# Small results two to a PSUM bank, and turns of rows at other places, in a fused attention and mixture-of-experts kernel

## The chip, the cores and the metric

The kernel runs on one core of a Trainium2 chip. The metric is the device time of one execution in microseconds (us); the time of a kernel is the median over its runs. In what follows PE is TensorE, DVE is VectorE, ACT is ScalarE, POOL is GpSimd and SP is SyncE; a "turn" is a transpose on PE.

## The reference

`x` is 2048 tokens (16 blocks of 128) of 256 numbers; the context has the same shape. First a gated attention with 16 heads in a sliding window, then a gated mixture of 8 experts, of which each token takes two. Cut to what matters:

```python
x = x + tanh(g_xattn) * attention(layernorm(x), ctx, ctx)
x = x + tanh(g_ffn) * moe(layernorm(x))

# attention: q = (x Wq + bq) / 4, k, v from ctx; a block of 128 queries sees
# its own block and the one before, inside a band of 129 keys
scores = where(valid, q @ k.T, -inf)
out = (softmax(scores) @ v) @ Wo + bo

# moe
xn = layernorm(x) * ln_gamma + ln_beta
probs = softmax(clip(xn @ Wr.T, -1e4, 1e4))
top_p, top_i = top_k(probs, 2)          # each token goes to two experts
# tokens in order take a slot each of their experts, at most 640 an expert
buf[e, slot] = xn[token]
g, u = split(buf[e] @ W12[e].T)         # 1024 + 1024
y = (silu(g) * u) @ W3[e].T             # back to 256
out[token] += y[slot] * weight          # for both of its experts
```

## The kernel before

All arithmetic is in float32 but for a few bfloat16 masks. The order of work on each engine is written by hand (a manual schedule): instructions stand on an engine in the order in which the Python code issues them, and the tile framework adds only the semaphores. PSUM, PE's output memory, has eight banks of 2 KB a partition. During the attention they are dealt out like this: `ps_m` has two banks that go round among nearly all small results (tag "m"), `ps_s` has two tiles of two banks for scores, `ps_t` has one tile of two banks for turned probabilities (`pp` of L524, read by ACT's `prT` copy, L526). After the attention loop another pool, `pf`, takes the place of `ps_s` and `ps_t`.

**Head.** Context, queries, keys and values of the first blocks are made. `unit_v(0, (0, 1))` makes the first values: its result `pv` (L437) is a tile of `ps_m`, and ACT's copies of the keys (`keo`, L370) free those banks.

**The attention loop** (L896 on) goes over the blocks t = 0 to 15. A round interleaves the attention of block t with later steps of earlier blocks and earlier steps of later ones. What follows is the middle of a round, with the functions that the change touches:

- DVE: `summed` (L513, the second half of the sums of exponents), `inverted` (L517, reciprocal `rd`), `divided(t-1)` (L567, `oT` from the products of the round before and `rb`), then the maxima (`largest`, L494) of block t+1.
- PE: `scores(t+1)`, `turned(t, 0)` (L524), `facing(t-2)` (L625: turns the normalised block `xn` into `pxt`; ACT copies it to `x2T`, L629), `attended(t-1)` (L575: the output projection `pp`; DVE adds it to `x_all`, L583, and takes the statistics of the second layernorm).
- `ranked` and `placed` for some rounds (L749: the slots of a group of routed blocks), then one of `units(t)`: `one()` makes keys, values, queries or turned blocks of later groups (L360, L437, L395).
- PE: `turned(t, 1)`, `routed(t-2)` (L635: router logits `pl` from `x2T`; DVE clips them into `logits`, L642), `by_head(t)` (L533: `prd`, turned reciprocals; DVE copies them to `rdT`), `weighted(t)` (L546 and L557: probabilities times values, `po`).
- `scaled(t-1)`: the second layernorm on POOL and DVE (L595, L602, L611, L612), which ends in `xn`; then POOL sends four of the waiting rows to their slots with indirect DMAs (L807).

Before the change every one of `pxt`, `pp`, a unit's result, `pl`, `prd` is a tile of its own in the two banks of `ps_m`, so each waits for the read of the result two before it.

**Head of the experts.** After the loop the last blocks are routed, while PE already makes gate and up products of the first expert (`gate_or_up`, L1009; `silu`, L1018; `hidden`, L1023) from its first three tiles of rows, which were fetched inside the loop. `ranked` (L749) follows DVE's choice of the top two (L734), and `send` issues the last indirect DMAs.

**Experts** are taken in the order 2, 0, 5, 1, 3, 4, 6, 7 (loop at L1397). An expert has up to five tiles ("slots") of 128 rows, and a switch on its count picks an arm of code with `m` slots. The first expert (`FIRST`) has m = 5 in this run: its down products (`down`, L1305 on) for slots 0 to 2 come first, then `slots_turned` (L1141) turns slots 3 and 4 (L1146, copied by ACT at L1158), then `up` (L1166) makes their gate and up products. The second and the third expert have m = 2 (`up`), the other five use `seven` (L1234, a scheme with seven products of half-matrices in place of eight), which needs sums of the turned rows (`row_sums`, L1226 on, DVE).

A down product of one slot is eight matmuls with two halves (`down_parts`, L1305): it yields after four matmuls, after eight, and then `weigh` (L1325) scales by the router's weight on DVE. At the boundary between two experts slots 0 to 3 of the next expert are turned (L1146, copied by ACT at L1151), then comes a half of a down product of the old expert, then the turn of slot 4 and `row_sums`, and then the remaining three halves:

```python
next(downs[0])
if i + 1 < E:
    slots_turned(nxt[0], bufT, 4, 5, halves=True)
    row_sums(bufT, bs)
for k, parts in enumerate(downs):
    ...
```

For the first expert `downs` has one product only. The weighted rows are added to the result in HBM by indirect DMAs of POOL (L1340), four copies move the result to the output.

Of the kernel before, what the change touches and what calls it, by code (L numbers as in the profile page):

```python
# [20 lines left out]
P = 128  # L21
D = 256
# [9 lines left out]
E = 8  # L32
# [22 lines left out]
def flamingo_block(  # L55
# [252 lines left out]
    with tc.tile_pool(name="grp", bufs=2) as grp, tc.tile_pool(  # L308
# [118 lines left out]

            return evict

        def unit_v(g, bs):  # L430
            cg, vp = ctxs[g], vps[g % 2]
            vpv = vp.rearrange("p b (k a) (h d) -> p b k a h d", a=2, h=2)
            n = len(bs)
            pv = ps_m.tile([P, n, D], F32, tag="m", name=f"pv_{g}_{bs[0]}")
            for i, b in enumerate(bs):
                for c in range(DC):
                    nc.tensor.matmul(  # L437
                        pv[:, i, :],
                        lhsT=cg[:, c, b * P : (b + 1) * P],
                        rhs=wv_sb[:, c, :],  # L440
                        start=(c == 0),
                        stop=(c == DC - 1),
                    )
# [68 lines left out]
        def summed(t, q, sc):  # L512
            nc.vector.tensor_reduce(sc[3][:, q, :, :], sc[2][q], AX.X, ALU.add)  # L513

        def inverted(t, sc):
            rd = small.tile([P, H], F32, tag="rd", name=f"rd_{t}")
            nc.vector.reciprocal(rd, sc[3].rearrange("p q i j -> p (q i j)"))  # L517
            return rd
# [8 lines left out]
            return prT  # L527


        def by_head(t, rd):  # L530

            prd = ps_m.tile([H, P], F32, tag="m", name=f"prd_{t}")
            nc.tensor.transpose(prd, rd, ident)  # L533
            rdT = wk.tile([H, P], F32, tag="rdT", name=f"rdT_{t}")
            nc.vector.tensor_copy(rdT, prd)
            return rdT
# [18 lines left out]
        def divided(t, po, rd):  # L555
            for oc in range(DC):
                nc.tensor.matmul(  # L557
                    po[:, 1, oc, :],
                    lhsT=sel[:, oc, :, :, :].rearrange("k s a d -> k (s a d)"),
                    rhs=rd,  # L560
                    start=True,
                    stop=True,
                )
            rb = wk.tile([P, DC, P], F32, tag="rb", name=f"rb_{t}")
            nc.scalar.copy(rb, po[:, 1, :, :])
            oT = wk.tile([P, DC, P], F32, tag="oT", name=f"oT_{t}")
            nc.vector.tensor_tensor(oT, po[:, 0, :, :], rb, ALU.mult)  # L567
            return oT

        def attended(t, oT):  # L570
            g, b = divmod(t, GB)
            x1 = xs[g][:, b, :]
            pp = ps_m.tile([P, D], F32, tag="m", name=f"pp_{t}")
            for c in range(DC):
                nc.tensor.matmul(  # L575
                    pp,
                    lhsT=oT[:, c, :],
                    rhs=wo_sb[:, c, :],
                    start=(c == 0),
                    stop=(c == DC - 1),  # L580
                )

            nc.vector.scalar_tensor_tensor(x1, pp, tgx[:, 0:1], x1, ALU.mult, ALU.add)  # L583
# [11 lines left out]
            nc.gpsimd.tensor_tensor(rs, ve, minus_half[:, 0:1], ALU.pow)  # L595
            return mv, rs
# [21 lines left out]
                )  # L618
            return normed

        def facing(t):
            g, b = divmod(t, GB)
            pxt = ps_m.tile([P, DC, P], F32, tag="m", name=f"pxt_{t}")
            for c in range(DC):
                nc.tensor.transpose(  # L625
                    pxt[:, c, :], xn2s[g][:, b, c * P : (c + 1) * P], ident
                )
            x2T = wk.tile([P, DC, P], F32, tag="x2T", name=f"x2T_{t}")
            nc.scalar.copy(x2T, pxt)  # L629
            return x2T  # L630

        def routed(t, x2T):
            pl = ps_m.tile([P, E], F32, tag="m", name=f"pl_{t}")
            for c in range(DC):
                nc.tensor.matmul(  # L635
                    pl,
                    lhsT=x2T[:, c, :],
                    rhs=wr_sb[:, c, :],
                    start=(c == 0),
                    stop=(c == DC - 1),  # L640
                )
            nc.vector.tensor_scalar(  # L642
                logits[:, t, :], pl, CLAMP, -CLAMP, ALU.min, ALU.max
            )
# [199 lines left out]
        with tc.manual_schedule(engines={PE, ACT, DVE}):  # L844
# [18 lines left out]
                normed_x(0, bs, *m)  # L863
            nc.vector.tensor_scalar(bqs, bq_sb, HD**-0.5, None, ALU.mult)
            nc.vector.tensor_copy(bvb, bv_sb.unsqueeze(2).to_broadcast([P, DC, P]))
            unit_v(0, (0, 1))()
            unit_k(1, 0)()
            unit_t(0)()
            normed_x(1, every, *measured(1, every))
# [26 lines left out]
            for t in range(NB):  # L896
# [4 lines left out]
                if t == 0:  # L901
                    prTs = [turned(t, 0, sc)]
                    unit_t(1)()
                    scn = scores(t + 1)
                    summed(t, 1, sc)
                    rdT = by_head(t, inverted(t, sc))
                    for q in range(2):
                        largest(t + 1, q, scn)
                else:
                    summed(t, 1, sc)  # L910
                    rd = inverted(t, sc)
                    oT = divided(t - 1, *pend)
                    if nxt:
                        scn = scores(t + 1)
                        for q in range(2):
                            largest(t + 1, q, scn)
                    prTs = [turned(t, 0, sc)]
                if t >= 2:
                    x2T = facing(t - 2)
                if t >= 1:  # L920
                    norm = attended(t - 1, oT)
                if routing is not None:
                    place = placed(*ranked(*routing))
                    next(place)
# [6 lines left out]
                    g, b = divmod(t - 1, GB)  # L931
                    mv_rs = measured(g + 2, [b])
                prTs.append(turned(t, 1, sc))
                if t >= 2:
                    routed(t - 2, x2T)
                if t >= 1:
                    rdT = by_head(t, rd)
                po = weighted(t, prTs, rdT)
                pend = po, rdT
                if t == 13:  # L940
# [98 lines left out]

            t = NB - 1  # L1040
            oT = divided(t, *pend)
            x2T = facing(t - 1)
            gate_or_up(0, 0)
            norm = attended(t, oT)
            silu(0)
            routed(t - 1, x2T)
            gate_or_up(0, 1)
            c = chosen(t - 4, 4)
            next(c)
# [7 lines left out]
            hidden(1)  # L1057
            silu(2)
            routing = next(c)
            x2T = facing(t)  # L1060
            gate_or_up(2, 1)
            routed(t, x2T)
            ranks = ranked(*routing)
            hidden(2)
            for _ in placed(*ranks):
# [14 lines left out]
            gate_or_up(5, 0)  # L1080
            routing = next(c)
            hidden(4)
            ranks = ranked(*routing)
            count = counted("count")
            for _ in placed(*ranks):
                pass
            for u in of_tiles(*routing[0:2]):
                send(*u)
            gate_or_up(5, 1)
            silu(5)  # L1090

            over = small.tile([P, E], F32, name="over", bufs=1)
# [12 lines left out]
    with tc.tile_pool(name="ffn", bufs=2, reuse_waits="tile") as ffn:  # L1105
# [271 lines left out]
        with tc.manual_schedule(engines={PE, ACT, DVE}):  # L1377
# [19 lines left out]
            for i, e in enumerate(ORDER):  # L1397
# [9 lines left out]
                for case in tc.Switch(nw, arms(e), hint=f"width_{e}"):  # L1407
# [24 lines left out]
                            slots_turned(rows, buf_a, s, min(s + 2, m, AT))  # L1432
                        up(w12, buf_a, None, 0, min(m, AT) * P)
                    for k, s in enumerate([*range(2, min(m, AT)), 0]):
                        down(e, w3, hT, rows, left, ysb, s, k)
                    if m == 2:

                        nc.tensor.matmul(
                            pys[1][:, 0:E], lhsT=ones, rhs=ones[:, 0:E], start=True, stop=True
                        )  # L1440
                    if m > AT:
                        slots_turned(rows, buf_b, AT, m, off=AT)
                        up(w12, buf_b, hT, AS, m * P, off=AS)
                    list(ahead)
                    for s in range(AT, m):
# [11 lines left out]
                downs = [down_parts(*args, 0, 1)] if e != FIRST else []  # L1457
                downs.append(down_parts(*args, 1, 0))
                next(downs[0])
                if i + 1 < E:  # L1460
                    slots_turned(nxt[0], bufT, 4, 5, halves=True)
                    row_sums(bufT, bs)
                for k, parts in enumerate(downs):
                    if k > 0:
                        next(parts)
                    next(parts)
                    if k + 1 < len(downs):
                        next(parts, None)
# [99 lines left out]
```

## Time and profile before

| | us |
|---|---|
| median of 3 runs (lowest to highest) | 528.17 (528.05 to 528.65) |
| profiled execution | 526.98 |
| its span, first to last instruction | 525.3 |
| PE busy in the span | 493.4 (94%) |
| DVE busy | 301.9 (57%) |
| ACT busy | 227.5 (43%) |
| POOL busy | 156.1 (30%) |
| granted TensorE clock, mean | 0.996 of full speed |

The profile is of one execution, 1.19 us below the median. Times in it are counted from the span's start. In lines of the timeline the first two numbers are start and duration in us, the name before the arrow is the tile written and those behind it are read; x8 joins eight instructions in a row; brackets at the end give the idle time of that engine just before, and what ended it. A name such as `ctx` or `x_all` can stand for a later tile that took over its memory. The attention loop lies at about 21 to 198, the head of the experts at 198 to 232, the experts at 232 to 516.

### The profile page before, as it was taken

How to read it: one execution, taken by the hardware profiler on the slowest of the kernel's cores; microseconds unless marked ns; L12 is line 12 of the kernel's file. 1: busy time of each engine (PE TensorE's matmuls, PEld its weight loads, DVE VectorE, ACT ScalarE, POOL GpSimd, SP SyncE). 2: the span in 40 equal slices, each digit the busy share in tenths (PEclk: the TensorE clock that was granted, in tenths of full speed). 3: DMA queues.
4: the chain of work that ended last, by engine and by line, in shares of the span. 5: the costliest groups of instructions: out<-in, count | busy, mean ns of one | idle time of the engine just before them, and what ended most of it. 6: DMA issues, size and time to landing. Idle time of an engine off the chain costs nothing.

```text
span 525.3 us, 8420 instructions
## 1 busy us (share of the span) xinstructions
PE 493.4 (94%) x2935; PEld 371.1 (71%) x2935; DVE 301.9 (57%) x748; ACT 227.5 (43%) x620; POOL 156.1 (30%) x187
## 2 busy tenths in 40 slices
PE   8998999999998889999999999999999999999993
PEld 4655666666666666578878888898677867877682
DVE  6578788877687966624453656373464256334510
ACT  3677777668665664311221242351441144024400
POOL 5133422254216255600222223323110211034212
PEclk9999999999999999999999999999999999999998
DMA  8999610011002116230477583572910250023301
GB/s 253 317 273 386 208 41 1 2 41 62 2 1 104 53 42 241 87 125 2 111 231 204 147 279 69 130 218 29 304 18 12 35 143 10 3 36 82 149 12 40
DMA packets 38410, 59.17 MB, mean 113 GB/s; under 512 B 3617, under 2 KB 33825, under 8 KB 36193
## 3 DMA queue, kind: packets, MB, share of 16 engines
q1 hardware_dynamic: 30704, 47.71, 27.3%
q0 software_dynamic: 7056, 10.24, 10.3%
q8 instruction: 42, 0.69, 0.5%
q14 instruction: 64, 0.52, 0.3%
q10 hardware_dynamic: 544, 0.00, 0.1%
HBM read 39.40 MB, written 19.34 MB: 112 GB/s over the span
## 4 chain that ended last, share of the span: by engine, by line
PE 70%; issue 8%; DVE 7%; ACT 6%; DMA 5%; POOL 1%; SPq 0%; ACTq 0%; POOLq 0%; DVEq 0%
PE py L1314 14%; PE pg L1258 9%; PE pu L1258 7%; PE pg L1172 4%; DMA acc_d<-ysb,tok 4%; PE pp L524 4%; PE pu L1172 4%; PE ps L482 3%; PE pq L411 3%; ACT prT L526 3%; PE po L546 3%; PE bank L1258 3%; PE ps L474 3%; PE pk L360 3%; DVE mx L494 2%
## 5 line engine op out<-in xcount | busy, mean ns | idle before, releaser
L1340 POOL DMA_INDIRECT acc_d<-ysb,tok x35 | 56.1, 1602 | 190.7 <-DMA acc_d<-ysb,tok 73.0
L1314 PE MATMUL py<-w,hT 128*128 128x256 f32 x432 | 97.1, 379 | 0.0
L1314 PEld LDWEIGHTS py<-w,hT 128*128 128x128 f32 x432 | 80.9, 190 | 11.2 <-DVE hT L1269 0.5
L505 ACT ACTIVATE pr<-ps,mx 128x128 f32<-128x128 f32 x256 | 69.5, 405 | 2.6 <-DVE mx L494 2.5
L1258 PE MATMUL pg<-bufT,w 128*128 128x320 f32 (+1 forms) x160 | 50.6, 398 | 0.2
L526 ACT COPY prT<-pp 128x1024 f32<-128x1024 f32 x32 | 32.6, 1019 | 40.0 <-PE pp L524 30.5
L513 DVE TENSOR_REDUCE sm<-pr 128x8 f32<-128x1024 f32 x32 | 38.9, 1217 | 14.1 <-ACT pr L505 14.1
L494 DVE TENSOR_REDUCE mx<-ps 128x8 f32<-128x1024 f32 x32 | 37.6, 1216 | 7.9 <-PE ps L482 7.7
L524 PE MATMUL pp<-ident,pr 128*128 128x128 f32 x256 | 34.6, 278 | 2.2 <-ACT prT L526 1.7
L807 POOL DMA_INDIRECT slot_d<-xn,slot x32 | 31.6, 988 | 14.5 <-issue 7.7
L524 PEld LDWEIGHTS pp<-ident,pr 128*128 128x128 f32 x256 | 28.2, 141 | 10.6 <-issue 6.0
L1258 PEld LDWEIGHTS pg<-bufT,w 128*128 128x128 f32 x160 | 28.0, 189 | 10.6 <-ACT vp L1292 2.3
L1151 ACT COPY bufT<-bank 128x256 f32<-128x256 f32 (+1 forms) x42 | 11.4, 347 | 51.8 <-PE bank L1146 45.1
L595 POOL TENSOR_TENSOR rs<-ve,minus_half 128x1 f32<-128x1 f32 x16 | 8.9, 556 | 78.7 <-DVE ve L591 78.6
L546 PE MATMUL po<-prT,vp 128*32 128x128 f32 x512 | 22.3, 277 | 7.1 <-DVE logits L642 2.9
L1289 ACT ACTIVATE vp<-pu 128x320 f32<-128x320 f32 (+1 forms) x40 | 15.8, 396 | 29.1 <-PE pu L1258 14.5
L1328 DVE TENSOR_SCALAR ysb<-py,rows 128x256 f32<-128x256 f32 x20 | 9.6, 482 | 31.2 <-PE py L1314 28.6
L1278 ACT COPY pg<-pg 128x320 f32<-128x320 f32 (+1 forms) x20 | 7.3, 367 | 42.7 <-PE pg L1258 36.8
L1184 ACT ACTIVATE vp<-pg 128x256 f32<-128x256 f32 x24 | 9.2, 383 | 37.2 <-PE pg L1172 34.9
L546 PEld LDWEIGHTS po<-prT,vp 128*32 128x32 f32 x512 | 14.7, 109 | 13.6 <-DVE logits L642 6.4
L1294 DVE TENSOR_TENSOR pu<-pg,vp 128x320 f32<-128x320 f32 (+1 forms) x20 | 8.9, 446 | 17.5 <-PE pg L1258 14.0
L482 PE MATMUL ps<-keo,qT 32*128 32x256 f32 x256 | 18.3, 400 | 0.0
(217 smaller groups left out, 967.2 us busy)
## 6 DMA issues: line engine op xcount, KB each, us to landing
w<-in_w12T_dram SPq DMA_DIRECT2D x16, 1024.0 KB, 8.3
w<-in_w3T_dram SPq DMA_DIRECT2D x8, 1024.0 KB, 12.3
slot_d<-zrow SPq DMA_DIRECT2D x1, 5300.0 KB, 26.6
rows<-slot_d SPq DMA_DIRECT2D x7, 662.5 KB, 4.2
x_all<-in_x_dram SPq DMA_DIRECT2D x4, 512.0 KB, 6.3
acc_d<-x_all SPq DMA_DIRECT2D x4, 512.0 KB, 4.6
out_dram<-acc_d SPq DMA_DIRECT2D x4, 512.0 KB, 8.1
ctx<-in_ctxT_dram SPq DMA_DIRECT2D x3, 512.0 KB, 6.1
```

The lines of the kernel that those rows point to most:

```text
L482: nc.tensor.matmul(pss[s // 2][:, s % 2, 2 * oc : 2 * oc + 2, :], lhsT=qT[rows, oc, b * P : (b + 1) * P], rhs=keo[rows, oc, b, :, :], star ...
L494: nc.vector.tensor_reduce(mx, sc[0][q], AX.X, ALU.max, negate=True)
L505: nc.scalar.activation(prs[q][:, i, j, :], pss[q][:, i, j, :], AF.Exp, bias=mxs[q][:, i, j : j + 1],)
L513: nc.vector.tensor_reduce(sc[3][:, q, :, :], sc[2][q], AX.X, ALU.add)
L524: nc.tensor.transpose(ppt[:, i, j, :], sc[2][q][:, i, j, :], ident)
L526: nc.scalar.copy(prT, ppt)
L546: nc.tensor.matmul(po[32 * s : 32 * s + 32, 0, oc, :], lhsT=vp[:, b, h, :], rhs=prTs[s // 2][:, s % 2, 2 * oc + a, :], start=(a == 0), sto ...
L807: d = nc.gpsimd.indirect_dma_start(out=slot_d, out_offset=bass.IndirectOffsetOnAxis(ap=slot[:, k, t : t + 1], axis=0), in_=xn2s[g][:, b, : ...
L1172: nc.tensor.matmul(ps, lhsT=w12[:, c, f0 : f0 + P], rhs=(buf[:, c, :, 0 : n // 2] if len(buf.shape) == 4 else buf[:, c, lo - off : hi - off]),
L1258: nc.tensor.matmul(to, lhsT=lhs[:, i * P : (i + 1) * P], rhs=rhs[:, 0:n], start=start, stop=True, skip_group_check=not start,)
L1314: mm = nc.tensor.matmul(py, lhsT=h, rhs=w3[:, f, :], start=(f == 0), stop=(f == FC - 1),)
L1340: nc.gpsimd.indirect_dma_start(out=acc_d, out_offset=bass.IndirectOffsetOnAxis(ap=tok[:, s : s + 1], axis=0), in_=ysb[:, s, :], in_offset= ...
```

## The change

1. `unit_v(0, (0, 1))` takes its PSUM tile from `ps_t` (tile `pv_0`).
2. In the loop, `facing` and `attended` write into two halves of one bank (`large_bank`), `routed` and `by_head` into two parts of another (`small_bank`). Matmuls and reads are separate functions now: first both groups of matmuls, then both reads.
3. At t = 15 `divided(14)` stands ahead of the last `summed` on DVE.
4. `gate_or_up(5, 1)` stands ahead of the last `ranked` and `counted`.
5. For the first expert with m > 3, the turn of slots 3 and 4 stands between the two halves of the down product of slot 0.
6. Between experts, where there are two down products, all of the first (with its `weigh`) stands ahead of the turn of slot 4 and `row_sums`; the second follows.

```diff
-        def unit_v(g, bs):
+        def unit_v(g, bs, pv=None):
...
-            pv = ps_m.tile([P, n, D], F32, tag="m", name=f"pv_{g}_{bs[0]}")
+            if pv is None:
+                pv = ps_m.tile([P, n, D], F32, tag="m", name=f"pv_{g}_{bs[0]}")
...
-            unit_v(0, (0, 1))()
+
+            pv = ps_t.tile([P, DC, GT], F32, tag="t", name="pv_0")
+            unit_v(0, (0, 1), pv[:, 0, :].rearrange("p (b d) -> p b d", d=D))()
...
+        def small_bank(t):
+            both = ps_m.tile([P, BANK], F32, tag="m", name=f"small_{t}")
+            return both[:, 0:E], both[0:H, P : 2 * P]
...
+        def large_bank(t):
+            both = ps_m.tile([P, 2, D], F32, tag="m", name=f"large_{t}")
+            return both[:, 0, :].rearrange("p (c t) -> p c t", c=DC), both[:, 1, :]
...
-            pp = ps_m.tile([P, D], F32, tag="m", name=f"pp_{t}")
...
-            pxt = ps_m.tile([P, DC, P], F32, tag="m", name=f"pxt_{t}")
...
-            pl = ps_m.tile([P, E], F32, tag="m", name=f"pl_{t}")
...
                 else:
+                    if not nxt:
+                        oT = divided(t - 1, *pend)
                     summed(t, 1, sc)
                     rd = inverted(t, sc)
-                    oT = divided(t - 1, *pend)
                     if nxt:
+                        oT = divided(t - 1, *pend)
                         scn = scores(t + 1)
...
-                if t >= 2:
-                    x2T = facing(t - 2)
                 if t >= 1:
-                    norm = attended(t - 1, oT)
+                    pxt, pp = large_bank(t)
+                    if t >= 2:
+                        facing(t - 2, pxt)
+                    attended(t - 1, oT, pp)
+                    if t >= 2:
+                        x2T = facing_read(t - 2, pxt)
+                    norm = attended_read(t - 1, pp)
...
-                if t >= 2:
-                    routed(t - 2, x2T)
                 if t >= 1:
-                    rdT = by_head(t, rd)
+                    pl, prd = small_bank(t)
+                    if t >= 2:
+                        routed(t - 2, x2T, pl)
+                    by_head(t, rd, prd)
+                    if t >= 2:
+                        routed_read(t - 2, pl)
+                    rdT = by_head_read(t, prd)
...
+            gate_or_up(5, 1)
             ranks = ranked(*routing)
             count = counted("count")
...
-            gate_or_up(5, 1)
             silu(5)
...
-                        down(e, w3, hT, rows, left, ysb, s, k)
+                        parts = down_parts(e, w3, hT, rows, left, ysb, s, k)
+                        next(parts)
+                        if s == 0 and m > AT:
+                            slots_turned(rows, buf_b, AT, m, off=AT)
+                        for _ in parts:
+                            pass
...
                     if m > AT:
-                        slots_turned(rows, buf_b, AT, m, off=AT)
                         up(w12, buf_b, hT, AS, m * P, off=AS)
...
                 next(downs[0])
+                if len(downs) > 1:
+                    next(downs[0])
+                    next(downs[0], None)
                 if i + 1 < E:
                     slots_turned(nxt[0], bufT, 4, 5, halves=True)
                     row_sums(bufT, bs)
-                for k, parts in enumerate(downs):
-                    if k > 0:
-                        next(parts)
-                    next(parts)
-                    if k + 1 < len(downs):
-                        next(parts, None)
+                if len(downs) > 1:
+                    next(downs[1])
+                next(downs[-1])
```

More of the change, by code (lines that the diff above doesn't have):

```diff
@@ L527, in turned, with by_head, by_head_read @@
             return prT
-        def by_head(t, rd):
-            prd = ps_m.tile([H, P], F32, tag="m", name=f"prd_{t}")
+        def small_bank(t):
+            both = ps_m.tile([P, BANK], F32, tag="m", name=f"small_{t}")
+            return both[:, 0:E], both[0:H, P : 2 * P]
+        def by_head(t, rd, prd):
             nc.tensor.transpose(prd, rd, ident)
+            return prd
+        def by_head_read(t, prd):
             rdT = wk.tile([H, P], F32, tag="rdT", name=f"rdT_{t}")
@@ L568, in divided, with attended @@
             return oT
-        def attended(t, oT):
-            g, b = divmod(t, GB)
-            x1 = xs[g][:, b, :]
-            pp = ps_m.tile([P, D], F32, tag="m", name=f"pp_{t}")
+        def large_bank(t):
+            both = ps_m.tile([P, 2, D], F32, tag="m", name=f"large_{t}")
+            return both[:, 0, :].rearrange("p (c t) -> p c t", c=DC), both[:, 1, :]
+        def attended(t, oT, pp):
             for c in range(DC):
@@ L581, in attended, with attended_read @@
                 )
+            return pp
+        def attended_read(t, pp):
+            g, b = divmod(t, GB)
+            x1 = xs[g][:, b, :]
             nc.vector.scalar_tensor_tensor(x1, pp, tgx[:, 0:1], x1, ALU.mult, ALU.add)
@@ L619, in scaled, with facing @@
             return normed
-        def facing(t):
+        def facing(t, pxt):
             g, b = divmod(t, GB)
-            pxt = ps_m.tile([P, DC, P], F32, tag="m", name=f"pxt_{t}")
             for c in range(DC):
@@ L627, in facing, with facing_read @@
                 )
+            return pxt
+        def facing_read(t, pxt):
             x2T = wk.tile([P, DC, P], F32, tag="x2T", name=f"x2T_{t}")
@@ L630, in facing, with routed @@
             return x2T
-        def routed(t, x2T):
-            pl = ps_m.tile([P, E], F32, tag="m", name=f"pl_{t}")
+        def routed(t, x2T, pl):
             for c in range(DC):
@@ L641, in routed, with routed_read @@
                 )
+            return pl
+        def routed_read(t, pl):
             nc.vector.tensor_scalar(
@@ L905, in flamingo_block @@
                     summed(t, 1, sc)
-                    rdT = by_head(t, inverted(t, sc))
+                    rdT = by_head_read(t, by_head(t, inverted(t, sc), small_bank(t)[1]))
                     for q in range(2):
@@ L1041, in flamingo_block @@
             oT = divided(t, *pend)
-            x2T = facing(t - 1)
+            x2T = facing_read(t - 1, facing(t - 1, large_bank("last")[0]))
             gate_or_up(0, 0)
-            norm = attended(t, oT)
+            norm = attended_read(t, attended(t, oT, large_bank("out")[1]))
             silu(0)
-            routed(t - 1, x2T)
+            routed_read(t - 1, routed(t - 1, x2T, small_bank("last")[0]))
             gate_or_up(0, 1)
@@ L1059, in flamingo_block @@
             routing = next(c)
-            x2T = facing(t)
+            x2T = facing_read(t, facing(t, large_bank("end")[0]))
             gate_or_up(2, 1)
-            routed(t, x2T)
+            routed_read(t, routed(t, x2T, small_bank("end")[0]))
             ranks = ranked(*routing)
```

## The prediction, made before the run

> **What bounds the kernel now.** I read the busy shares and the chain that ended last on the page, then the list of what TensorE (PE) waited for, and then the timeline around each of those waits that the diff touches.
>
> ```profile
> PE 493.4 (94%) x2935; PEld 371.1 (71%) x2935; DVE 301.9 (57%) x748; ACT 227.5 (43%) x620; POOL 156.1 (30%) x187
> ...
> PE 70%; issue 8%; DVE 7%; ACT 6%; DMA 5%; POOL 1%; SPq 0%; ACTq 0%; POOLq 0%; DVEq 0%
> ```
>
> PE is busy 94% of the 525.3 us span, and the chain lies on it for 70%. The change adds and removes no matmul, and no DMA changes its place in SP's or POOL's queue, so it can only give back PE's 32 us of idle time, or add to them. The waits of PE (total us, times, longest):
>
> ```profile
> PE po L546 <- DVE logits L642: 2.9, 4, 0.8
> PE bank L1146 <- ACT bufT L1151: 1.9, 2, 1.3
> ...
> PE pp L575 <- DVE oT L567: 1.1, 1, 1.1
> ...
> PE pv L437 <- ACT prT L526: 0.9, 1, 0.9
> PE pg L1172 <- ACT ctx L1158: 0.7, 1, 0.7
> PE rank L749 <- DVE top L734: 0.7, 1, 0.7
> PE pv L437 <- ACT keo L370: 0.7, 1, 0.7
> PE rank L749 <- ACT x2T L629: 0.6, 2, 0.3
> PE pt L395 <- ACT x2T L629: 0.6, 2, 0.3
> PE pv L437 <- ACT x2T L629: 0.6, 2, 0.3
> ```
>
> Each of these lines answers to one part of the diff; together they are 10.7 us. The question is how much comes back: a wait that goes is worth only what the next event lets through. In what follows, gains are differences of start times in the profiled execution (526.98 us, 1.68 more than its span; 1.19 below the median of 528.17).
>
> **1. First value product in a bank of its own.** `pv` starts at 10.42 after waiting for the `keo` copy (L370); PE was free at 9.59, and its weights had landed at 9.04 (DMA issue at 3.14, 5.9 to landing). So it can start 0.83 earlier. The following `pk` at 12.26 reuses a bank already copied out, and ACT, which must copy `vp`, is busy with `keo` to 11.71 (8.93 + 2.78), the earliest end of the new `pv` being 11.6. I take 0.85 (the extra 0.02 is a launch gap), bounds 0.6 to 0.95.
>
> **2. Two results in one bank, in the loop.** Facing (`pxt`, L625) and attended (`pp`, L575) now share a bank, both matmul groups first, then both reads; routed (`pl`) and by_head (`prd`) likewise. The small result behind them therefore finds a free bank without waiting for the x2T copy. In exchange the x2T copy on ACT waits until attended's matmuls end, and the read of `pp` on DVE (L583) waits for the x2T copy. Queued behind these are ACT's exponents (L505) and the next `prT` copy, and on DVE the statistics and logits. Round t=2:
>
> ```profile
> 48.57 1.03 PE L575 MATMUL pp<-wo_sb,oT 128*128 128x256 f32 x4
> 49.46 0.38 ACT L629 COPY x2T<-pxt 128x256 f32<-128x256 f32 x1
> ...
> 49.79 0.47 DVE L583 SCALAR_TENSOR_TENSOR x_all<-pp,tgx,x_all 128x256 f32<-128x256 f32 x1
> ...
> 50.80 1.01 ACT L526 COPY prT<-pp 128x1024 f32<-128x1024 f32 x1
> ...
> 52.00 1.08 PE L546 MATMUL po<-prT,vp 128*32 128x128 f32 x32 [0.82 <-DVE logits L642]
> ```
>
> L575 ends at 49.60, so x2T starts at about 49.64 instead of 49.46: 0.18 later. L583 then starts at about 50.07 instead of 49.79: 0.28 later. DVE has 0.43 of idle time ahead of L513 at 52.88, which hides that; without this cover it would cost 0.28 a round. What of the 0.82 that `po` waited for logits? The line says that it goes, but the `prT` copy on which `po` also depends ends only at 51.81 and will end 0.18 later. So `po` starts at about 52.04: no gain but 0.04 lost, and the same at t=3 and t=4 (62.20, 72.39): -0.1 in all, bounds -0.6 to 0.
>
> PE's waits of 0.29 for x2T occur at t=5, 6, 7, 9, 10 and 11. At t=6 and 10 (`pv`) and 11 (`rank`) nothing else is late: 3 x 0.29 = 0.87. At t=5 and 9 the second half of `pt` lies in the shared bank and waits for L583, which ends 0.4 after the wait that goes; at t=7 `pk` does so, and L583 stands behind 2.34 us of maxima (L494). There I take nothing. At t=12 `pv` waited 0.87 (start 162.13) because the `prT` copy was late at 160.79; `pv` needs it no more: 0.75, but only 0.29 if that copy comes on time in the next execution. Sum of the loop: 0.87 + 0.75 - 0.1 = 1.52, bounds 0.3 to 2.4.
>
> [...]
>
> **3. Division ahead of the last sum (t=15).**
>
> ```profile
> 192.48 1.10 PE L575 MATMUL pp<-wo_sb,oT 128*128 128x256 f32 x4 [1.15 <-DVE oT L567]
> ...
> 195.40 0.57 POOL L595 TENSOR_TENSOR rs<-ve,minus_half 128x1 f32<-128x1 f32 x1
> ...
> 198.11 0.44 PE L625 MATMUL pxt<-ident,xn 128*128 128x128 f32 x2
> ```
>
> `oT` needs `rb` (ends 191.06) and not the sum L513 (190.55 to 191.77), so L575 can start at about 191.5: 0.95 earlier. But the end of this stretch is `facing` at 198.11, which waits for `xn` from POOL, and POOL's chain (195.40, `h` 196.51, `xn` 197.31 to 198.03) stands behind four sends (190.51 to 195.37) that are anchored in POOL's earlier work and don't move. All of PE's 0.95 turns into waiting at 198.11: 0, bounds 0 to 0.95.
>
> **4. A gate product ahead of the ranks.** `rank` at 216.74 waited 0.69 for DVE's top-2; four gate matmuls fill it now. But PE then reaches the down product earlier, and there ACT and DVE resume at 225.8 (after 4.98 and 5.48 idle, with inputs ready at 221.6 and 222.9, while indirect sends are under way). PE's matmuls on the last two hidden tiles, at 226.57 and 227.0, were just met (weight load waited 0.15). If these stay where they are, about 0.6 is waited there: 0.1, bounds -0.5 to 0.7. The ranks come 1.5 later, POOL's sends for them start at 221.74, and their slots were ready at 218.47: that covers it.
>
> **5. First expert's last slot turned within the down product.** The turn at 230.91 (0.60), ACT's copy (231.59, 0.58) and then `pg` at 232.23 with 0.72 waited stood behind one another. Sixteen down matmuls fill 223.98 to 230.91, 0.433 each. Now the turn comes after half a product, 4 x 0.433 = 1.73 earlier, with the rows landing at 228.57 by the neighbouring load; the copy is done under the other half. Gain 0.72 + 0.15 of gaps = 0.87, bounds 0.4 to 0.95.
>
> **6. Turns between experts.** A down matmul is two records here (x8 is four matmuls).
>
> ```profile
> 272.29 1.89 PE L1314 MATMUL py<-w,hT 128*128 128x256 f32 x8
> ...
> 275.45 0.44 PE L1146 MATMUL bank<-ident,rows 128*128 128x128 f32 x2 [1.27 <-ACT bufT L1151]
> ```
>
> ```profile
> 330.79 0.38 PE L1146 MATMUL bank<-ident,rows 128*128 128x128 f32 x2
> ...
> 331.01 5.35 PE L1314 MATMUL py<-w,hT 128*128 128x256 f32 x24
> ...
> 332.95 0.48 DVE L1231 TENSOR_TENSOR wq_sb<-bufT,x_all 128x320 f32<-128x320 f32 x1
> ```
>
> Four matmuls after 272.29 end at 274.02; slot 4's turn came at 275.45 because ACT's copies started late (274.75, after 3.62 idle): 1.43 lost. At 298.16 it is 0.83 in the same way. Eight matmuls (3.46) last past both: 1.43 + 0.83 = 2.26. The price is the cover behind: the row sums must be ready when the next expert starts. At 330.79 they took to 333.43, 2.64 after slot 4's turn; with the weighing (L1328, 0.5) now ahead of them 3.14, against 0.22 + 3.46 = 3.68 of remaining matmuls. It fits with 0.54 to spare: no cost, bounds 0 to 1.73 a boundary if not.
>
> **Sum.** 0.85 + 1.52 + 0 + 0.10 + 0.87 + 2.26 = 5.60. From 526.98 that is 521.4, and with the 1.19 to the median **522.6 us**. The tail after the last matmul (516.3 to 525.3) is untouched.
>
> **Rivals.**
> - *Only the experts count (0.21).* The loop and the head are paced by ACT's and POOL's chains, so parts 1 to 4 come to nothing; 5 and 6 leave 3.13: 525.0. For it: the four zeros that I already found. Against: at t=6, 10 and 11 I see no later event.
> - *More comes back (0.09).* POOL's and DVE's lateness at 195.4 and 225.8 belongs to one execution, and parts 3 and 4 give 0.95 + 0.6, with 0.87 at t=5, 7 and 9: 8.0, so 520.1.
> - *Slower (0.10).* Slot 4's copies run late at the five boundaries ahead of a `seven` expert, as ACT's copies did by 2 us or more at 274.75. It decides once the sums take more than 3.68 after the turn. With 2 us of lateness the cost is 2.0 - 0.54 = 1.46, five times 7.3: 1.7 worse than before, 529.9. Against it: at 331.21 ACT copied slot 4 at once.
> - *It doesn't do what it says (0.05).* The added waits (0.18 on ACT, 0.28 on DVE, some 13 rounds, up to 3.6) and a lost 1 to 2 in part 4 eat the gain: 528.
>
> **How the numbers follow.** The forecast keeps 0.55, with its own range of 521 to 524. A range of 520.0 to 526.1 takes in the first two rivals and leaves out the last two. Measurements of this kernel can tell about 0.2% (1.06 us) from no change: faster 0.85, same 0.05, slower 0.10.
>
> **What would show it.** Right: in the waits of PE the lines of `bank` for `bufT`, `pg` for `ctx`, `pv` for `keo` and those for x2T are gone; `po` at t=2 to 4 now waits for `prT`; a new wait stands at the `facing` of 198 and at the products of 226. Wrong: a new wait of the first matmul of `seven` for DVE's sums, or ACT idle ahead of the last `bufT` copies, or a loop round longer than before at t=2 to 11.

## The result, and the profile after

The changed kernel took 521.77 us (median of 4 runs, 521.42 to 522.34), beside 528.35 for the kernel before in the same runs: ratio 0.9877, 95% interval 0.9859 to 0.9894, so 6.5 us or 1.2% faster. The forecast was 522.6 with a range of 520.0 to 526.1. The profiled execution took 522.01 (span 520.3), 4.97 less than that of before; of the two, that of before happened to lie 1.4 under its median and that of after 0.2 above it.

The page after: PE is as busy as before, in a shorter span (15 of its records are missing from this trace).

```profile
PE 491.1 (94%) x2920; PEld 372.2 (72%) x2935; DVE 303.2 (58%) x748; ACT 228.6 (44%) x620; POOL 157.1 (30%) x187
```

What PE waited for (total us, times, longest):

```profile
PE po L554 <- ACT prT L527: 6.6, 15, 0.8
...
PE pt L395 <- DVE x_all L598: 1.1, 2, 0.5
PE large_last L639 <- POOL xn L627: 0.9, 1, 0.9
PE py L1345 <- DVE x_all L1054: 0.8, 1, 0.8
PE pk L360 <- DVE x_all L598: 0.5, 1, 0.5
```

Every line that was named as going is gone: `bank` for `bufT`, `pg` for `ctx`, `pv` for `keo`, all those for x2T, `po` for logits, and `rank` for DVE. What came in their place is the point of this view. The first line (15 waits, 6.6 us) says that the copies of probabilities on ACT (`prT`) now end last in nearly every round. The second and the last are waits that the shared bank adds (in rounds 5, 9 and 7), the third and the fourth the places where the division's and the gate product's gains stop.

Because all these executions have nearly the same work, the time can be followed by the starts of the same matmuls in both traces (before minus after, cumulative):

| up to | us gained |
|---|---|
| first scores (21.04 before) | 0.30 |
| last scores of the loop (179.68) | 2.34 |
| first gate product (198.39) | 2.18 |
| first down product (223.98) | 3.11 |
| first product on rows 3 and 4 (232.23) | 2.58 |
| second expert (257.60) | 2.69 |
| third expert (280.91) | 4.18 |
| fourth expert (304.10) | 4.93 |
| end of the span | 4.97 |

The wait that the shared bank adds, in round 2 (columns: start, duration, instruction, idle before it and its cause). x2T starts just after the projection ends, and the read of the projection after x2T:

```profile
48.29 1.03 PE L585 MATMUL large<-wo_sb,oT 128*128 128x256 f32 x4
49.35 0.37 ACT L646 COPY x2T<-large 128x256 f32<-128x256 f32 x1
49.76 0.48 DVE L598 SCALAR_TENSOR_TENSOR x_all<-large,tgx,x_all 128x256 f32<-128x256 f32 x1 [0.16 <-ACT x2T L646]
```

With the 0.28 by which this trace runs ahead here, that is 49.63 and 50.04 on the clock of before; the prediction had 49.64 and 50.07. Between experts the four copies still start late, but PE has eight matmuls to do (x16, two records each) and meets the next turn without waiting:

```profile
269.60 3.62 PE L1345 MATMUL py<-w,hT 128*128 128x256 f32 x16
...
271.53 1.20 ACT L1182 COPY bufT<-bank 128x256 f32<-128x256 f32 x4 [3.08 <-issue]
...
273.06 0.38 PE L1177 MATMUL bank<-ident,rows 128*128 128x128 f32 x2
```

### The profile page after: what moved, and what is told of

Read it like the earlier page. It is cut to its first block, busy times and chain, and to the rows that moved or that the text cites. A ratio compares the mean times of both kernels' runs of the same rounds, so it can differ in the third digit from the quotient of the medians.

```text
span 520.3 us, 8402 instructions
## 1 busy us (share of the span) xinstructions
PE 491.1 (94%) x2920; PEld 372.2 (72%) x2935; DVE 303.2 (58%) x748; ACT 228.6 (44%) x620; POOL 157.1 (30%) x187
## 4 chain that ended last, share of the span: by engine, by line
PE 71%; ACT 7%; issue 7%; DVE 7%; DMA 5%; POOL 1%; SPq 0%; POOLq 0%; DVEq 0%; ACTq 0%
PE py L1345 15%; PE pg L1289 9%; PE pu L1289 7%; PE pu L1203 4%; PE pg L1203 4%; PE pp L525 4%; DMA acc_d<-ysb,tok 4%; ACT pr L506 4%; PE ps L483 3%; PE pk L360 3%; ACT prT L527 3%; PE bank L1289 3%; DVE mx L495 2%; PE pv L438 2%; PE pq L411 2%
## 5 line engine op out<-in xcount | busy, mean ns | idle before, releaser
L554 PE MATMUL po<-prT,vp 128*32 128x128 f32 x512 | 23.7, 277 | 7.3 <-ACT prT L527 6.6
L475 PE MATMUL ps<-causal,ident_b 128*128 128x512 bf16 x49 | 15.8, 382 | 2.0 <-ACT pr L506 1.4
```

The costliest lines, as they stand in the source:

```text
L554: nc.tensor.matmul(po[32 * s : 32 * s + 32, 0, oc, :], lhsT=vp[:, b, h, :], rhs=prTs[s // 2][:, s % 2, 2 * oc + a, :], start=(a == 0), sto ...
```

## The experiments

Times are medians; each ratio is to the kernel before on the same chip, with its 95% interval. Effects here are 0.1 to 1%, so I read the ratio for the sum and the trace for the place. Of each edit the main lines are shown. "The stretch" is the time from PE's first down product to its first product on rows 3 and 4 (223.98 to 232.23 before, 8.25).

**1. The turns of rows alone** (parts 5 and 6 of the change's list). The edit to the kernel before is the hunks of the change for these parts, of which the main lines are:

```diff
+                        if s == 0 and m > AT:
+                            slots_turned(rows, buf_b, AT, m, off=AT)
...
+                if len(downs) > 1:
+                    next(downs[0])
+                    next(downs[0], None)
                 if i + 1 < E:
                     slots_turned(nxt[0], bufT, 4, 5, halves=True)
```

> The kernel before with parts 5 and 6 alone (turns of rows within and between experts' products). Theory (each wait of PE that goes is worth the difference of start times): 0.87 within the first expert plus 1.43 and 0.83 between experts, 3.1 us less than before, about 525.2. Rival (the lateness at the first expert belongs to ACT's and DVE's pause near 226 and stays): the 2.26 between experts alone.

Measured: ratio 0.9936 (0.9911 to 0.9962), 3.4 us. The stretch is 7.34 beside 8.23 in *head_only*, which has the old order there: 0.89. The wait ahead of the product on rows 3 and 4, before and here (the turn, then the product):

```profile
232.23 1.13 PE L1172 MATMUL pg<-ctx,w 128*128 128x256 f32 x4 [0.72 <-ACT ctx L1158]
```

```profile
227.22 0.60 PE L1146 MATMUL bank<-ident,ctx 128*128 128x128 f32 x4
...
229.38 1.03 PE L1172 MATMUL pg<-ctx,w 128*128 128x256 f32 x4
```

From the second expert to the fourth it took 44.51 against 46.50: 1.99. How late the copies of the old order are differs from execution to execution (45.99 in *shared_only*, which has the old order too). The theory holds; the rival's 2.26 without the first expert's part does not, for that part shows its 0.89.

**2. The shared banks alone** (part 2), with all of its hunks, of which two lines are:

```diff
+                    pxt, pp = large_bank(t)
...
+                    pl, prd = small_bank(t)
```

> The kernel before with part 2 alone (two results to a bank in the loop). Theory (the gain of a round is the gap of starts, 0.46 to 0.56 in rounds 6, 10, 11, 0.74 in round 12, minus 0.25 in rounds 5 and 9): 2.0 us by the last scores of the loop, of which at most 0.3 is lost by the first expert, so 1.7 to 2.0 less than before. Rival (the loop's end is paced by POOL's sends, so the gain turns into waiting for the last normalised blocks): under 0.8 less.

Measured: ratio 0.9951 (0.9933 to 0.9970), 2.6 us. From the first to the last scores 154.76, and 156.56 to 156.57 in each of the three kernels of this set that have the old loop: 1.81 gained, 1.7 of it still there at the first gate product. The rival (under 0.8) is out.

**3. The head alone** (part 1).

```diff
-            unit_v(0, (0, 1))()
+            pv = ps_t.tile([P, DC, GT], F32, tag="t", name="pv_0")
+            unit_v(0, (0, 1), pv[:, 0, :].rearrange("p (b d) -> p b d", d=D))()
```

> The kernel before with part 1 alone (the first value product in a bank of its own). Theory (a wait of 0.83 goes, and the loads come when they come): 0.5 to 0.85 less than before; in the profile no idle time of PE ahead of the first pv, whenever the first keys begin. Rival (the 0.30 seen in the changed kernel is all that there is, since ACT's copies are next): 0.3 or less, with ACT late for the following key copies.

Measured: ratio 0.9990 (0.9971 to 1.0008), 0.5 us and not told from none. In the trace PE no longer idles ahead of `pv`, but the first keys began at 6.39, later than in the others, and `pv` came at 10.21. Over all profiles the first scores start at 20.48 on average in nine executions with part 1 (20.05 to 20.78) and at 20.88 in four without (20.68 to 21.04): 0.4, between theory and rival. But these executions differ in when the first keys are done, and the part on why the prediction was right shows that with this taken out the theory's 0.83 is there.

**4. Division and gate product alone** (parts 3 and 4).

```diff
+                    if not nxt:
+                        oT = divided(t - 1, *pend)
                     summed(t, 1, sc)
...
+            gate_or_up(5, 1)
             ranks = ranked(*routing)
```

> The kernel before with parts 3 and 4 alone (division ahead of the last sum; a gate product ahead of the ranks). Theory (0.95 of the division is given back at the facing product behind POOL's sends, 0.69 of the ranks is mostly given back at the down product, where ACT and DVE resume late): 0 to 0.4 less than before. Rival (the waits go for good): 1.0 to 1.6 less.

Measured: ratio 0.9978 (0.9962 to 0.9994), 1.2 us. Half of each, of theory and rival: from the last scores to the first gate product 19.15 against 19.19 in *head_only*, so the division gives 0.04; from there to the first down product 24.65 against 25.60, and the stretch unchanged (8.22 against 8.23), so the gate product gives 0.95 and keeps it. What the theory relied on there, that ACT and DVE resume late, didn't happen in this set of runs at all (below).

**5. The changed kernel again, as a base.**

> The changed kernel as it is, on the chip of this set of runs, as the base for the three beside it. Theory (the parts add up): 2.0 to 2.6 of the shared banks, 3.1 to 3.4 of the turns, 0.3 to 0.5 of the head and about 1.0 of the ranks make 6.4 to 7.5 us less than the kernel before, and the profile shows no pause of ACT and DVE near 222, so that the gate product's gain is kept. Rival (the division and the gate product run into POOL's sends and the down product): 5.5 or less.

Measured: 520.94, ratio 0.9890 (0.9867 to 0.9913), 5.8 us (4.6 to 7.0): between theory and rival, and the interval reaches into both. The four kernels with parts alone add up to 7.6, but on another chip and each known to about 1 us only. The wait at the facing product (0.85) and a pause of ACT and DVE near 222 are both back.

**6. One send fewer in round 14.**

```diff
-                    pace(normed, 4)
+                    pace(normed, 3 if t == 14 else 4)
```

> The changed kernel with three sends of rows in place of four in round 14, the fourth left for the end. Theory (PE's wait of 0.86 for the last but one normalised block is made by the four sends ahead of it on POOL, and it is where the division's gain went): the wait goes and the kernel is 0.7 to 0.9 us faster than the changed one. Rival (DVE's statistics or the later sends take their place, or the wait comes back at the next normalised block): the same within 0.2.

Measured: ratio 0.9866 (0.9844 to 0.9889), 0.7 us under the base of its set by the medians (1.3 by the ratios), which the intervals alone can't tell from none. The trace can:

```profile
192.19 0.57 POOL L610 TENSOR_TENSOR rs<-ve,minus_half 128x1 f32<-128x1 f32 x1 [0.40 <-issue]
...
194.89 0.44 PE L639 MATMUL large_last<-ident,xn 128*128 128x128 f32 x2
```

POOL stands idle ahead of the norm's first step (0.40) instead of sending, PE's wait is gone, and the way from the last scores to the first gate product is 17.98 instead of 18.76. So the four sends were where the division's gain went; the division and one send fewer together bring 0.8, the division alone nothing. One send fewer without the division was not run.

**7. Banks not shared in rounds 5, 7 and 9**, on top of 6.

```diff
-                    pxt, pp = large_bank(t)
+                    if t in (5, 7, 9):
+                        pxt = ps_m.tile([P, DC, P], F32, tag="m", name=f"pxt_{t}")
+                        pp = ps_m.tile([P, D], F32, tag="m", name=f"pp_{t}")
+                    else:
+                        pxt, pp = large_bank(t)
```

> The kernel pace_3 with separate banks for the two large results in rounds 5, 7 and 9, where the next product needs the second of the two banks. Theory (there sharing costs 0.25 in rounds 5 and 9 and nothing in 7, since the next product waits for the projection's read, which waits for the x2T copy): 0.5 us faster than pace_3. Rival (the probabilities' copies on ACT set the pace of these rounds anyway): the same as pace_3 within 0.2.

Measured: ratio 0.9870 (0.9847 to 0.9892), no difference to *pace_3* by time. In the trace rounds 5 and 9 take 11.19 each, as before the change, and 11.44 in *pace_3*: 0.5, as expected, and round 7 the same. The gain is seen, the time can't resolve it.

**8. Less cover between experts.** Slot 4 is turned after 12 matmuls of 16.

```diff
                 if len(downs) > 1:
                     next(downs[0])
                     next(downs[0], None)
+                    next(downs[1])
                 if i + 1 < E:
                     slots_turned(nxt[0], bufT, 4, 5, halves=True)
                     row_sums(bufT, bs)
-                if len(downs) > 1:
-                    next(downs[1])
                 next(downs[-1])
```

> The changed kernel with slot 4 turned after 12 matmuls instead of 8, so that four matmuls (1.73) are left behind it. Theory (the row sums need 3.14 after the turn, and 1.95 of cover is left): PE waits about 1.2 ahead of each of the five experts that use seven, 6 us slower than the changed kernel. Rival (the first products of an expert do not need the sums at once): under 2 us slower.

Measured: ratio 0.9963 (0.9950 to 0.9977), 3.9 us slower than *after_again*: between the two. From the start of one expert that uses `seven` to the next it took 33.81 and 33.63 for the first two of them (32.22 and 32.19 in *after_again*), and 0.3 to 0.5 more for each of the others. At the start of the fifth expert:

```profile
330.85 0.48 DVE L1262 TENSOR_TENSOR wq_sb<-bufT,x_all 128x320 f32<-128x320 f32 x1
...
331.27 0.52 PE L1289 MATMUL bank<-x_all 128*128 128x192 f32 x2
...
331.98 0.30 ACT L1309 COPY pg<-pg 128x192 f32<-128x192 f32 x1 [2.40 <-PE bank L1289]
...
332.33 0.59 PE L1289 MATMUL pg<-bufT,w 128*128 128x192 f32 x2 [0.54 <-ACT pg L1309]
...
334.82 0.59 PE L1289 MATMUL pg<-x_all 128*128 128x192 f32 x2 [0.56 <-DVE pu L1325]
```

The sums end at 331.33, after the expert's first product has begun (330.67), and yet they are not what PE waits for: its first product on a sum (331.27) starts without a wait, as the rival had it. PE waits for ACT's copy of that expert's first result, and then for DVE (the bracket at 331.98 names a product of PE, the event that came last by the profile). ACT's branch into the new arm of code is at 329.33, behind its copies of slot 4, and its next instruction at 331.84; DVE's branch is at 330.80, behind the sums, and its next instruction at 333.82. In *after_again* ACT's branch is at 327.41 and its next instruction at 330.55, DVE's 328.89 and 331.84, and PE does not wait. So four matmuls are too short a cover and eight are enough, but what they have to cover is the branches of ACT and DVE (2.5 to 3.1); the sums count in that DVE's branch stands behind them.

**9. The gate product behind the ranks again** (part 4 undone).

```diff
-            gate_or_up(5, 1)
             ranks = ranked(*routing)
...
+            gate_or_up(5, 1)
             silu(5)
```

> The changed kernel with part 4 alone undone (the gate product behind the ranks again). So far five profiles with both part 4 and part 5 show ACT and DVE pausing near 222 and PE 8.6 to 8.8 from the first down product to the next expert part, against 7.3 with part 5 alone. Theory (part 4 brings 1.0 up to the down product and the pause takes 1.3 of it back): the pause is gone, the stretch is about 7.3, and the kernel is the same as the changed one within 0.5 us. Rival (the pause is a matter of the single execution, or of the chip): the stretch stays at 8.7 and the kernel is about 1 us slower.

Measured: ratio 0.9880 (0.9858 to 0.9902), as the changed kernel (0.9877 and 0.9890). PE's wait for the ranks is back (0.68), the stretch is 7.63 beside 8.65 in *after_again*: what part 4 brings to the first down product, it loses behind it. But the pause did not go, as the theory expected it to: ACT and DVE resume at 224.72. PE only comes later to it. (In this execution the granted clock was 0.50 from 195.65 to 199.06, about 1.5 lost, so its span is not read.)

**10. Without the last block's two sends.**

```diff
-            for u in of_tiles(*routing[0:2]):
-                send(*u)
             silu(5)
```

> The changed kernel without the two sends of the last block's rows, which are left out of the computation (their slots stay empty, counts and widths are the same). Theory (PE's completions reach ACT and DVE late because the sends' traffic or their issue holds something that these need): the last send ends 2.5 us earlier and the pause ends as much earlier or vanishes; the stretch is 7.3 to 7.6, about 1.2 us faster. Rival (the pause belongs to PE's branch and its fetch of code after it): ACT and DVE resume at the same time after PE's branch, about 4.0, and the stretch stays at 8.6 to 8.8.

Measured: ratio 0.9837 (0.9813 to 0.9860), some 2 to 3 us under the changed kernel's two ratios. The changed kernel first, then this one (the last send, ACT's next step, and PE's down products):

```profile
220.88 0.96 POOL L826 DMA_INDIRECT slot_d<-xn,slot  x1 [0.30 <-issue]
223.79 0.49 ACT L1049 ACTIVATE vp<-pg 128x384 f32<-128x384 f32 x1 [5.24 <-PE py L1345]
...
224.42 3.22 PE L1345 MATMUL py<-w,x_all 128*128 128x256 f32 x12 [0.79 <-DVE x_all L1054]
```

```profile
218.10 0.96 POOL L826 DMA_INDIRECT slot_d<-xn,slot  x1 [0.30 <-issue]
220.64 5.34 PE L1343 MATMUL py<-w,x_all 128*128 128x256 f32 x24
220.75 0.49 ACT L1049 ACTIVATE vp<-pg 128x384 f32<-128x384 f32 x1 [1.78 <-PE pg L1040]
```

The last send starts 2.78 earlier, ACT resumes 3.04 earlier although PE's branch into the expert's arm of code is at the same place (219.69 and 219.57), and the stretch is 7.34. ACT follows the sends, not the branch.

**11. Part 4 undone on top of 7**, so the edits of 6, 7 and 9 together.

> The kernel pace_3_unshared with part 4 undone. Theory (the pause costs more than part 4 brings): 0.3 us faster than pace_3_unshared, about 0.0133 under the kernel before by ratio, with the stretch at 7.3. Rival (part 4 is worth its 1.0): about 1 us slower than pace_3_unshared.

Measured: 520.15, ratio 0.9843 (0.9822 to 0.9865), the lowest of the complete kernels, but in another set than *pace_3_unshared* (0.9870), and the intervals overlap. From the first gate product to the product on rows 3 and 4 it took 33.15, and 33.37 in *pace_3_unshared*: 0.2 less, near the theory's 0.3, and the rival is out. The stretch is 7.65 and not 7.3, since the pause is there too. That it beats the kernel before by 1.6% is measured; that it beats the changed one is likely (0.9843 against 0.9877 and 0.9890) and not shown beside it.

## Why the prediction was right, point by point

| part | predicted | seen |
|---|---|---|
| 1 head | 0.85 | 0.30 in the pair; 0.83 with the keys done alike |
| 2 loop | 1.52 | 1.81 alone, 2.03 in the pair of profiles |
| 3 division | 0 | 0.04 alone, -0.15 in the pair |
| 4 gate product | 0.10 | 0.95 without the pause, about -0.2 with it |
| 5 first expert | 0.87 | 0.89 without the pause, 0.60 with it |
| 6 between experts | 2.26 | 2.25 in the pair, 1.99 alone |

In the pair of profiles the sum is 4.97 and not 5.60: the head gave 0.55 less, the loop 0.5 more, parts 4 and 5 together 0.40 in place of 0.97. That the total came near is in part luck: the loop's surplus offsets what the head lacks, and the two profiled executions, 4.97 apart, lie differently to their medians, which are 6.5 apart.

*Head.* The mechanism and the size held; what was not priced is that PE's first keys are not done at the same pace in every execution. Before, and in *pace_3_unshared*, where they run alike:

```profile
6.15 3.60 PE L360 MATMUL pk<-ctx,wk_sb 128*128 128x512 f32 x8
10.42 2.00 PE L437 MATMUL pv<-wv_sb,ctx 128*128 128x256 f32 x8 [0.68 <-ACT keo L370]
```

```profile
6.10 3.60 PE L360 MATMUL pk<-ctx,wk_sb 128*128 128x512 f32 x8
9.54 1.89 PE L438 MATMUL pv<-wv_sb,ctx 128*128 128x256 f32 x8
```

From the first key product to `pv` that is 4.27 and 3.44, so 0.83 is gained; the 0.02 of a launch gap in the term of 0.85 is shown by no run. In the changed kernel it is 3.8: its key products begin at 6.40, and the second follows the first after 0.82 in place of 0.43. In all thirteen traces PE's products, from the second on, follow each other every 0.85 until the trace's record of the full granted TensorE clock begins, and every 0.43 behind that where nothing else holds them. It begins at 5.89 before, at 5.80 in *pace_3_unshared* and at 7.17 in the changed kernel. Where it began early (4.17 in *cover_4*, 4.50 in *no_gate*), the keys had to wait in their middle (0.83 between two of them; the profile names the load of the context), and it took 4.15 and 4.14; *late_only*, without part 1, is of the same kind with 4.57. What sets the moment at which the clock rises was not tried; it spreads from 4.17 to 7.27 with part 1 and from 4.87 to 5.89 without.

*Loop.* The mechanism held, the size was off in two terms of opposite sign (+0.8 and -0.5). I priced the x2T rounds by the idle figure in the brackets (0.29), where I had priced the experts by starts. Round 6, before and after:

```profile
91.66 1.99 PE L437 MATMUL pv<-wv_sb,ctx 128*128 128x256 f32 x8 [0.29 <-ACT x2T L629]
```

```profile
91.15 1.89 PE L438 MATMUL pv<-wv_sb,ctx 128*128 128x256 f32 x8
```

The projection starts at 90.33 and at 90.28, so `pv` follows 1.33 later before and 0.87 later after: 0.46 gained, and 0.56 with the 0.10 by which `pv` itself is shorter (1.83 and 1.73 to the turns behind it). Rounds 6, 10, 11 gave 0.56 each (1.68, not 0.87). Rounds 5 and 9 lost 0.25 each where I had 0: the next product takes the bank that the projection's read leaves, and that read now waits for x2T (`pt` for L598, 1.1 in two). Round 12, priced at 0.75, gave 0.75 in the pair and 0.55 in *shared_only*; the 2.03 of the pair also holds 0.26 of round 8, in which the execution of before happened to be late. Rounds 2 to 4 gave 0 within 0.02, for the reason named: `po` now waits for `prT`. The order of the two reads of a shared bank is in the trace (0.16 of waiting for x2T in round 2); it costs 0.5 in the two rounds where the bank is wanted next, and not the 3.6 that the last rival allowed for.

*Division.* Right, with the cause: pacing one send fewer gave 0.8.

*Gate product.* The term of 0.10 came from a trace with the pause. There the measured one is about -0.2: *pace_3_unshared* is 0.84 shorter up to the down product than *no_gate_both*, which is the same kernel without part 4, and its stretch is 1.06 longer (8.71 and 7.65). So a little more than what is gained ahead of the pause is lost behind it, within the bounds given. In *late_only*, without the pause, part 4 keeps its 0.95, above the upper bound of 0.7: I took the pause for a feature of the code and had no price for its absence.

*Experts.* Right in both sizes: the turn's wait went, and the cover of eight matmuls was enough. The third expert comes 21.82 after the second in all nine profiles with part 6, and 22.96 to 23.31 in the four without; on the way to the fourth up to 0.9 comes back as a wait of PE for which the profile names no other engine ("issue"). The reason for the cover was wrong: the row sums need not be ready when the next expert starts. In *cover_4* it is ACT's and DVE's branches that no longer fit behind the turn. The slower rival (late last copies) did not occur; with four matmuls less it would have cost 0.3 to 1.6 a boundary.

The rival "only the experts count" fell with *shared_only*, and "it doesn't do what it says" with the waits' list; "more comes back" was true for the ranks in one set of runs and for the division never.

## What to carry to other kernels

Price a removed wait by the starts of the two neighbours in the trace, not by the idle figure in brackets: ends are modelled, and here the figure was 0.29 where 0.46 was to be had. Then look for the event that is next to last; where it belongs to a queue with its own pace (four sends on POOL here), the gain waits for that queue: the division gave 0.04 alone, and 0.8 with one send less. Where an engine branches into other code, count its branch (2.5 to 3.1 here, at the boundaries in question) in what has to be covered. Two results in one bank paid where nothing wanted that bank next (0.56 a round in rounds 6, 10 and 11), and cost where it was wanted (0.25 in rounds 5 and 9); choose round by round.

## What the runs showed that was not expected

ACT and DVE heard of PE's work late while rows were being sent. In nine of the thirteen profiles (before, after, and seven of the experiments) ACT's last `silu` of the first expert's head started 1.7 to 2.1 after POOL's last indirect send ended, though its input had been ready for up to 4 us; in the changed kernel the trace has no completion of PE between 218.04 and 223.71, and then seven within 0.4. In the other four, all of one set of runs on one chip, `silu` ran 1.1 to 2.0 before that send's end, at once when its input was there. This is such an execution; the last send is the second line:

```profile
220.95 0.49 ACT L1018 ACTIVATE vp<-pg 128x384 f32<-128x384 f32 x1 [2.09 <-PE pg L1009]
221.07 0.96 POOL L807 DMA_INDIRECT slot_d<-xn,slot  x1 [0.30 <-issue]
```

Taking two sends away moved the resumption with them (the last send 2.78 earlier, ACT 3.04), so the sends are part of the cause; why one set of runs is free of it (the chip or something else), and what is held back, stays open. The same set is also free of a lateness of ACT in round 13 (a `prT` copy 1.5 to 1.6 late before and after, none in *shared_only*), where four sends are under way as well.

The late copies between experts are another matter. At the second boundary ACT's branch out of the expert's arm is at 270.76 before the change, and its next instruction at 273.80; after it 268.07 and 270.57. In between the trace has DMA packets of 8 KB that the profile calls `instruction` (from 272.23 before, from 269.09 after). Of ACT's 32 branches in the two traces, 20 have such a packet between the branch and the next instruction, and 2.43 to 3.04 pass there; the other 12 have none, and 0.40 to 0.47 pass. ACT's and DVE's branches in *cover_4* are of the first kind (packets from 330.25 and 332.04, 2.5 and 3.0 passed). That the engine waits for these packets was not tried.
